# Probabilities and queries of the DRAM exchange read together, and a rearranged start of the attention loop

## The chip, the core and the metric

The kernel runs on one core of a Trainium2 chip. A core has five engines with instruction streams of their own: TensorE (PE in the profile; its weight loads are a row of their own, PEld), VectorE (DVE), ScalarE (ACT), GpSimd (POOL) and SyncE (SP), which only issues transfers. A transfer (DMA) is issued by SP, ScalarE or GpSimd and is carried out by 16 DMA engines that all queues share. On each engine the instructions run in the order in which they were written; between engines they wait on semaphores. The metric is the device time of one execution in microseconds (us).

## The reference

```python
x = x + L0_ffn(L0_cond(x, ...))     # an adapter product, then a layer with two of eight experts
x = x + L1_ffn(L1_cond(x, ...))     # attention, then a layer with sixteen of 64 experts

# L1_cond for 8 sequences of 128 tokens, 32 query heads, 8 key heads, head size 128
q = rope(rmsnorm(x @ Wq.T)); k = rope(rmsnorm(x @ Wk.T)); v = x @ Wv.T
kc, vc = k_cache[block_table], v_cache[block_table]   # 16 pages of 32 tokens: 512 cached keys
scores = q @ concat(kc, k).T / sqrt(128)              # 640 keys; four query heads share a key head
scores[cached keys past the sequence's length] = -1e30
o = softmax(scores) @ concat(vc, v)
return o @ Wo.T
```

All is in 32-bit floats. Time goes to the attention: the projections, 256 score products of 128 x 640, their softmax, the products with the values, and the output projection.

## The kernel before

**Units.** One sequence with one key head and its four query heads is a *unit*; there are 64. Two units of one sequence are a *step* (the code's `st`, 32 of them). The loop at the end runs one `iteration(u)` for each unit and three more; iteration u does the scores of unit u, and beside it the values of unit u-2, the output product of unit u-3, the projection of a later pair of units, and the norms and rotation of unit u+3. "Turn u" in this text is iteration u.

**A unit's way.** `project` (L261) makes queries, keys and values on TensorE, and VectorE adds the parts up (L264). ScalarE squares and sums each head (`norms`, L310), GpSimd makes 1/rms of it (`ss` L314, `rs` L316). VectorE rotates (`rotate_q`, `rotate_k`, L342 and after) with a table that GpSimd makes for each step (`make_tables`, L235; two buffers). The rotated queries and key must then be transposed: head size on the partitions. For the scores `heads_qk` (ScalarE, L906) puts them into `qkT`. For each of four heads, TensorE makes a 128 x 640 score in a PSUM bank (L837, L840; two such banks), VectorE masks it, takes the minimum and so frees the bank (L850, the row name is a custom operation), ScalarE makes the exponential and its sum (L861), VectorE the reciprocal, GpSimd the normalized probability (L867), and VectorE transposes it in blocks of 32 x 32 into the buffer `pb` (`blocks`, L872).

**The exchange through DRAM.** VectorE's transpose turns only within blocks of 32 x 32. The blocks themselves change places by a round through DRAM. The buffer `pb` of iteration u holds, for each of four quarters, 640 numbers of the four heads' probabilities of unit u (`PW`) and 160 of the rotated queries and key of unit u+2 (`XW = PW + 160`), which `blocks_qk` (L823) puts there. `exchange_out` writes it to DRAM in four transfers (L886): quarters 0 and 1 by SP, 2 and 3 by ScalarE. At the head of the next iteration, `exchange_in` on SP reads it back in two transfers: first the queries into `qkb` (L896), then the probabilities into `pT` (L899):

```python
if u + 2 in range(3, NU):
    qkb = wk1.tile([P, QD, NH * 32], F32, tag="qkb", name=f"qkb_{u + 2}")
    nc.sync.dma_start(out=qkb, in_=m[:, :, PW:])
    qkb_t[u + 2] = qkb
pT = wk1.tile([P, QD, PW], F32, tag=f"pT{u % 2}", name=f"pT_{u}")
nc.sync.dma_start(out=pT, in_=m[:, :, :PW])
```

`qkb` is used at the end of the same iteration by `heads_qk` for the next unit's scores, and `pT` by `values` (L919) at the end of the iteration after. There is one `pb` buffer: `blocks_qk` of the next iteration, which comes at its third head, waits until the write from it has landed. Units 0 to 2 take another way in part: the queries of units 0 to 2 are transposed on TensorE ahead of the loop, and iterations 0 and 1 use the memory of `pT0` and `pT1` as `pb`; the queries of unit 3, which go with iteration 1, lie in a gap of the buffer `xo` and have four transfers of their own.

**Other transfers.** SP also loads the key pages of the next step (`gather`, L196; 16 pages of 32 KB each): pages 0 to 9 in the step's first iteration and 10 to 15 in its second, three of them ahead of the exchange's read and the others behind it. GpSimd gathers the value rows by an indirect transfer (`gather_v`, L206, two an iteration) and issues the weight loads.

**Order.** The order on every engine is the order of the code (`manual_schedule`): no planner moves anything. Semaphores are set by the framework. Transfers issued by SP and ScalarE signal one of eight semaphores, in turn by the order of the code, and a transfer also waits for the one before it on the same semaphore.

**Sums.** TensorE's work is cut by forming sums of weights and inputs (fewer products of larger sums, after Strassen and Winograd). GpSimd makes most of them: of `xo` in `sums_x` (L172 to L176), of the projection's weights in `sums_q` (L166), of the output's weights in `sums_o` (L994), each in a slot "(iteration, head)" given by tables.

Of the kernel before, what the change touches and what calls it, by code (L numbers as in the profile page):

```python
# [9 lines left out]
F32 = mybir.dt.float32  # L10
I32 = mybir.dt.int32
AF = mybir.ActivationFunctionType
# [4 lines left out]
P = 128  # L17
B = 8
S = 128
# [4 lines left out]
D = 128  # L24
HKV, REP = 8, 4
NH = REP + 1
PAGES, PSIZE, NPP = 64, 32, 16
# [3 lines left out]
GH = 2  # L31
NQ = HKV // GH
HW = NH // 2 * D + D
QD = P // 32
HN = DM // 2
PW = REP * (LC + 1) * 32
XW = PW + NH * 32
# [21 lines left out]
def adaln_ffn_kernel(  # L59
# [169 lines left out]
    def make_tables(st):  # L229

        b = st % B
        t = pj.tile([P, 2, 4, D // 2], F32, tag="tab", name=f"tab_{st}", bufs=2)
        nwv = nw.rearrange("p i (t d) -> p (i t) d", t=2)
        for i, f in enumerate((cos, sin)):
            nc.gpsimd.tensor_tensor(  # L235
                t[:, i], nwv, f[:, b, :].unsqueeze(1).to_broadcast([P, 4, D // 2]), ALU.mult
            )
        tab_t[st] = t
# [64 lines left out]
    def norms(u):  # L303

        cs, b = c_t[u], units[u][0] % B
        ss = pj.tile([P, NH], F32, tag="ss", name=f"ss_{u}", bufs=5)
        sq = pj.tile([P, D], F32, tag="sq", name=f"sq_{u}")
        for h in range(NH):
            at = h // 2 * HW + h % 2 * D if h < REP else 2 * D
            nc.scalar.activation(sq, cs[:, at : at + D], AF.Square, accum_out=ss[:, h : h + 1])  # L310
        vn = pj.tile([P, D], F32, tag="vn", name=f"vn_{u}", bufs=6)
        nc.scalar.activation(vn, cs[:, 2 * HW - D :], AF.Copy, scale=down[:, b : b + 1])
        vn_t[u] = vn
        nc.gpsimd.tensor_scalar(ss, ss, 1.0 / D, eps[:, b : b + 1], ALU.mult, ALU.add)  # L314
        rs = pj.tile([P, NH], F32, tag="rs", name=f"rs_{u}", bufs=5)
        nc.gpsimd.tensor_tensor(rs, ss, mhalf, ALU.pow)  # L316
        rs_t[u] = rs
# [31 lines left out]
    def rotate(u):  # L349
        rotate_q(u)  # L350
        rotate_k(u)
# [46 lines left out]
    with ExitStack() as l0:  # L398
# [217 lines left out]
        for t in range(B):  # L616
            l0_adapter(t, True)
            if t >= 1:
                l0_turn_low(t - 1)
            l0_adapter(t, False)  # L620
            if t + 3 < B:
                l0_load(t + 3)
            if t + 2 < B:
                l0_load_x(t + 2)
            if t in (3, 4):
                load_q(t - 3)
            if 2 <= t <= 5:
                gather(0, (t - 2) * 4, (t - 1) * 4)
            elif t > 5:
                gather(1, (t - 6) * 4, (t - 5) * 4)  # L630
            if t >= 2:
                l0_turn(t - 2)

            if t == 5:
                project_whole(0, 0, 0, 1)
                norms(0)
            if t == 6:
                project_whole(0, 0, 1, 0)
            if t == 7:
                project_whole(0, 1, 1, 1)  # L640
                transpose_qk(0)
            if t >= 1:
                l0_experts(t - 1)
            l0_base(t)
            if t == 0:
                l0_rows()
            if 1 <= t <= 4:
                l0_angles(t - 1)
            if t in (3, 6):
                gather_v(t // 3 - 1, 0, LC)  # L650
            if t in (5, 6):
                make_tables(t - 5)
            if t == 4:
                project_whole(0, 0, 0, 0)
            if t == 5:
                project_whole(0, 0, 1, 1)
                sums_q(nc.vector, 0, 3, 2)
            if t == 6:
                project_whole(0, 1, 0, 1)
                rotate(0)  # L660
                norms(2)
                sums_q(nc.vector, 0, 4)
            if t == 7:
                project_whole(0, 1, 0, 0)
                norms(1)
# [2 lines left out]
        project_whole(0, 1, 1, 0)  # L668
        l0_turn(B - 2)
        rotate(1)  # L670
        l0_experts(B - 1)
        project_whole(1, 0, 0, 0)
        transpose_qk(1)
# [117 lines left out]
    with ExitStack() as l1:  # L791
# [6 lines left out]
        )  # L798

        p_t, pb_t, pT_t, den_t, o_t, oT_t, y_t = {}, {}, {}, {}, {}, {}, {}  # L800
        mask_t, px_t, qkb_t, qk_out = {}, {}, {}, {}

        def make_mask(st):
            b = st % B
# [4 lines left out]
        def new_pb(u):  # L809

            if u < 2:
                pb_t[u] = wk1.tile([P, QD, PW], F32, tag=f"pT{u}", name=f"pb_{u}")
                return
            pb_t[u] = wk1.tile([P, QD, XW], F32, tag="pb", name=f"pb_{u}")

        def blocks_qk(u, w):

            if w == 1:
                gap = xo[:, 0, 4:].rearrange("p x c s -> p (x c s)")[:, : NH * S]
                qk_out[w] = gap.rearrange("p (i f) -> p i f", i=QD)  # L820
            else:
                qk_out[w] = pb_t[w][:, :, PW:]
            nc.vector.transpose(  # L823
                qk_out[w].rearrange("p i (h a) -> p h i a", a=32),
                qk_t.pop(u).rearrange("p h t d -> p h (t d)").rearrange(
                    "p h (i a) -> p h i a", a=32
                ),
            )
# [40 lines left out]
        def blocks(u, h):  # L869

            w = (LC + 1) * 32
            nc.vector.transpose(  # L872
                pb_t[u][:, :, h * w : (h + 1) * w].rearrange("p i (j a) -> p j i a", a=32),
                p_t.pop((u, h)).rearrange("p (j i a) -> p j i a", i=QD, a=32),
            )

        def exchange_out(u):

            pb = pb_t.pop(u)
            m = dram_x.tile([QD, 32, QD, XW], F32, tag="px", name=f"px_{u}")  # L880
            w = XW if u + 2 in range(3, NU) else PW
            for i in range(QD):
                eng = nc.sync if i < QD // 2 else nc.scalar
                for n, end in ((PW, w), (0, PW)) if u == 1 else ((0, w),):
                    src = qk_out[u] if n else pb[:, :, :end]
                    (nc.sync if n else eng).dma_start(  # L886
                        out=m[:, :, i, n:end].rearrange("k b f -> b k f"),
                        in_=src[i * 32 : (i + 1) * 32],
                    )
            px_t[u] = m  # L890

        def exchange_in(u):
            m = px_t.pop(u).rearrange("k b i f -> (k b) i f")
            if u + 2 in range(3, NU):
                qkb = wk1.tile([P, QD, NH * 32], F32, tag="qkb", name=f"qkb_{u + 2}")
                nc.sync.dma_start(out=qkb, in_=m[:, :, PW:])  # L896
                qkb_t[u + 2] = qkb
            pT = wk1.tile([P, QD, PW], F32, tag=f"pT{u % 2}", name=f"pT_{u}")
            nc.sync.dma_start(out=pT, in_=m[:, :, :PW])  # L899
            pT_t[u] = pT  # L900

        def heads_qk(u):

# [48 lines left out]
        def slot(which, n):  # L952
# [21 lines left out]
            (1, 1): (T3, 0),  # L974
            (1, 2): (T3, 1),
            (2, 2): (T2, 0),
            (3, 0): (T2, 1),
            (3, 2): (T4, 0),
            (4, 0): (T4, 1),
            (7, 0): (T1, 0),  # L980
            (7, 1): (T1, 1),
        }
# [1 line left out]
        def sums_o(u, h):  # L984
# [11 lines left out]
        SUMS_X = {  # L996
            (0, 1): ((2, 0),),
            (0, 2): ((2, 1),),
            (6, 0): ((3, 0),),
            (7, 0): ((3, 1),),  # L1000
            (8, 0): ((0, 0),),
            (8, 1): ((0, 1),),
            (8, 2): ((1, 0),),
# [12 lines left out]
        def sums_w(u, h):  # L1016

            if u < 16:
                for i in SUMS_X.get((u, h), ()):
                    sums_x(*i)  # L1020
                do = {(3, 1): (0, 1), (4, 1): (1, 3), (4, 2): (1, 2), (5, 1): (1, 4), (5, 2): (1, 1)}
                if (u, h) in do:
                    sums_q(nc.gpsimd, *do[u, h])
            if u >= NU - 16:
                return
            r, g = u % 16, (u // 16 + 1) * GH
            do = {
                (11, 0): (0, 3),
                (11, 1): (0, 2),
                (11, 2): (0, 4),  # L1030
                (12, 0): (0, 1),
                (12, 2): (1, 3),
                (13, 1): (1, 2),
            }.get((r, h))
            if do is not None:
                sums_q(nc.gpsimd, g + do[0], do[1])
            if (r, h) in ((13, 1), (13, 3)):
                sums_q(nc.vector, g + 1, {1: 1, 3: 4}[h])
# [186 lines left out]
        def iteration(u):  # L1225
# [16 lines left out]
                slots = (1, 2, 6) if four else (4, 5, 3)  # L1242
            st = u // GH
            pages = on(u) and 1 < st + 1 < NQ * B
            first, end = ((0, 10), (10, NPP))[u % GH]
            if pages:
                gather(st + 1, first, first + 3)
            if on(u - 1):
                exchange_in(u - 1)
            if pages:  # L1250
                gather(st + 1, first + 3, end)
# [18 lines left out]
            for h in range(REP):  # L1270
                if on(u):
                    scores(u, h)
                    mask_exp(u, h)
                    if h > 0:
                        normalize(u, h - 1)

# [44 lines left out]
                norms(4 + u)  # L1321
            elif 5 < u + 3 < NU:
                norms(u + 3)
            if on(u):
                blocks(u, REP - 2)
                blocks(u, REP - 1)
                exchange_out(u)
# [187 lines left out]
```

## Time and profile before

| | |
|---|---|
| three runs, us | 1232.58, 1235.32, 1240.6; median 1235.32 |
| the profiled execution, us | 1228.33, of which the profile's span is 1226.5 |
| busy: TensorE, VectorE, GpSimd, ScalarE | 98%, 74%, 59%, 41% of the span |
| TensorE's granted clock | 1.0 of full speed over the whole |
| DMA | 302.71 MB, 247 GB/s on average; the 16 engines busy 73% from 120 to 200 us, 86% from 200 to 1150 us |
| the loop over units | first score at 115.4 us of the span, last at 1150.8 us |
| TensorE busy by stretch | 73.13 of the 80 us from 120 to 200; 942.28 of the 950 us from 200 to 1150 |

The busy times are the profile's first part. A row of a timeline gives the start in us from the span's start, the duration in us of the group from its first to its last instruction, the engine (SPq and ACTq are the instructions with which SP and ScalarE issue transfers), line, operation, output and input by their names in the program, and, in brackets, the idle time before it with what ended that. A row of the waits gives who waited (engine, output, line) for whom, then the total in us, how many times, and the longest.

### The profile page before, as it was taken

To read this page: it belongs to the slowest core of one execution; us is meant where nothing else is said; L and a number is where in the kernel's file an instruction comes from. 1 tells how busy PE (TensorE), PEld (TensorE's weight loads), DVE (VectorE), ACT (ScalarE), POOL (GpSimd) and SP (SyncE) were. 2 spreads that over 40 slices of the span, in tenths; PEclk is the share of its full clock that TensorE was granted. 3 is DMA by queue.
4 is the path that set the end of the run, shared out by engine and by line. 5 is a ranking of instruction groups with operands and counts; after the bars stand their busy time and mean duration, and the time that the engine had idled before them with its cause. 6 is when DMAs were issued, how large, how long until landed. Compare 5 with 4: busy or idle time off the path is not lost.

```text
span 1226.5 us, 16786 instructions
## 1 busy us (share of the span) xinstructions
PE 1202.6 (98%) x4159; PEld 709.2 (58%) x4159; DVE 909.9 (74%) x2098; ACT 503.7 (41%) x1457; POOL 721.2 (59%) x801
## 2 busy tenths in 40 slices
PE   8999989999999999999999999999999999999998
PEld 7765445565555556555556565655555555655444
DVE  2545877887988787878888787888787878876522
ACT  1344544444444444444344444444443444443211
POOL 2433868778755576677656675687556775732100
PEclk9999999999999999999999999999999999999999
DMA  8832688888888988898789888998889888888742
GB/s 306 286 101 96 205 253 251 247 272 275 261 245 251 280 259 237 294 288 287 236 263 294 281 231 270 297 289 248 246 257 287 262 255 262 263 260 235 219 126 97
DMA packets 206836, 302.71 MB, mean 247 GB/s; under 512 B 84819, under 2 KB 120404, under 8 KB 205844
## 3 DMA queue, kind: packets, MB, share of 16 engines
q1 hardware_dynamic: 174964, 208.72, 53.9%
q10 hardware_dynamic: 18720, 52.32, 15.9%
q0 software_dynamic: 13056, 40.60, 9.8%
q8 instruction: 33, 0.54, 0.2%
q14 instruction: 63, 0.52, 0.1%
HBM read 185.64 MB, written 115.93 MB: 246 GB/s over the span
## 4 chain that ended last, share of the span: by engine, by line
PE 68%; DMA 12%; DVE 6%; POOL 5%; issue 3%; SPq 3%; ACT 2%; ACTq 0%; DVEq 0%; POOLq 0%
PE o L919 15%; PE p L261 14%; PE s L837 12%; PE y L1044 10%; DMA px<-pb 9%; PE s L840 3%; PE bp L548 2%; PE op L1402 2%; DVE pb L872 2%; PE cp L526 2%; PE y L1057 2%; POOL p L867 2%; PE fz L733 2%; PE p L294 2%; POOL wqkv L166 1%
## 5 line engine op out<-in xcount | busy, mean ns | idle before, releaser
L861 ACT ACTIVATE p<-p,low 128x640 f32<-128x640 f32 x256 | 211.6, 827 | 463.1 <-DVE den L866 300.9
L867 POOL TENSOR_SCALAR p<-p,den 128x640 f32<-128x640 f32 x256 | 208.6, 815 | 270.2 <-DVE den L866 268.8
L261 PE MATMUL p<-wqkv,xo 128*128 128x384 f32 x784 | 282.3, 487 | 5.1 <-DVE c L264 4.9
L850 DVE CUSTOM_DVE_ANT_0 p<-s,mask,rs 128x640 f32<-128x640 f32 x256 | 222.0, 878 | 78.8 <-PE s L840 77.9
L837 PE MATMUL s<-kt,qkT 128*128 128x512 f32 x504 | 259.2, 596 | 8.5 <-DVE low L850 3.3
L919 PE MATMUL o<-pT,vt 128*128 128x512 f32 x512 | 230.2, 592 | 0.0
L872 DVE STREAM_TRANSPOSE pb<-p 128x640 f32<-128x640 f32 x256 | 211.0, 825 | 18.7 <-POOL p L867 18.7
L1044 PE MATMUL y<-wo,oT 128*128 128x256 f32 x784 | 206.6, 380 | 0.1
L261 PEld LDWEIGHTS p<-wqkv,xo 128*128 128x128 f32 x784 | 147.8, 190 | 75.9 <-DVE c L264 10.1
L840 PEld LDWEIGHTS s<-qkT 128*128 128x128 f32 x504 | 95.8, 190 | 120.5 <-issue 120.5
L206 POOL DMA_INDIRECT vt<-in_vc,vrow x128 | 143.3, 1120 | 33.8 <-issue 31.8
L919 PEld LDWEIGHTS o<-pT,vt 128*128 128x128 f32 x512 | 97.3, 190 | 110.3 <-issue 95.2
L837 PEld LDWEIGHTS s<-kt,qkT 128*128 128x128 f32 x504 | 93.4, 190 | 82.3 <-issue 34.3
L1044 PEld LDWEIGHTS y<-wo,oT 128*128 128x128 f32 x784 | 131.8, 191 | 8.9 <-PE s L840 0.2
L310 ACT ACTIVATE sq<-c 128x128 f32<-128x128 f32 x320 | 98.8, 309 | 8.1
L840 PE MATMUL s<-qkT 128*128 128x128 f32 x504 | 96.8, 274 | 0.0
L823 DVE STREAM_TRANSPOSE pb<-ca 128x640 f32<-128x640 f32 x60 | 50.3, 839 | 52.5 <-DMA px<-pb 51.5
L316 POOL TENSOR_TENSOR rs<-ss,mhalf 128x5 f32<-128x5 f32 x64 | 83.1, 1298 | 5.3
L942 ACT COPY oT<-o 128x512 f32<-128x512 f32 x64 | 37.5, 585 | 90.7 <-PE o L919 67.4
L919 PE MATMUL o<-pT,vn 128*128 128x512 f32 x128 | 65.4, 592 | 0.0
L314 POOL TENSOR_SCALAR ss<-ss,eps 128x5 f32<-128x5 f32 x64 | 21.6, 338 | 74.2 <-ACT sq L310 74.2
L264 DVE TENSOR_TENSOR c<-c,p 128x384 f32<-128x384 f32 x84 | 44.8, 534 | 22.5 <-PE p L261 22.4
(193 smaller groups left out, 1415.0 us busy)
## 6 DMA issues: line engine op xcount, KB each, us to landing
pT<-px SPq DMA_DIRECT2D x64, 1280.0 KB
px<-pb ACTq DMA_DIRECT2D x120, 400.0 KB
px<-pb SPq DMA_DIRECT2D x120, 400.0 KB
qkb<-px SPq DMA_DIRECT2D x61, 320.0 KB
kt<-in_kc SPq DMA_DIRECT2D x512, 32.0 KB
wqkv<-in_wqkv POOLq DMA_DIRECT2D x32, 384.0 KB, 5.3
wo<-in_wo POOLq DMA_DIRECT2D x17, 512.0 KB, 6.2
yd<-yp SPq DMA_DIRECT2D x12, 512.0 KB
```

The costliest lines, as they stand in the source:

```text
L206: nc.gpsimd.indirect_dma_start(out=kv_t[step][1][:, c, :], out_offset=None, in_=vc, in_offset=bass.IndirectOffsetOnAxis(ap=vrow[:, hf, at ...
L261: nc.tensor.matmul(out=ps, lhsT=xo[:, pr, x, c, :], rhs=w[:, c, :], start=(c == 0), stop=(c == 1))
L310: nc.scalar.activation(sq, cs[:, at : at + D], AF.Square, accum_out=ss[:, h : h + 1])
L316: nc.gpsimd.tensor_tensor(rs, ss, mhalf, ALU.pow)
L837: nc.tensor.matmul(out=s[:, :L], lhsT=qkT[:, h, :], rhs=kt[:, :, g % GH, :], start=True, stop=True)
L840: nc.tensor.matmul(out=s[:, L:NK], lhsT=qkT[:, h, :], rhs=qkT[:, REP, :], start=True, stop=True)
L850: nc.vector.tensor_tensor_reduce(out=p, in0=s_t.pop((u, h))[:, :NK], in1=mask_t[st], scale=rs_t[u][:, h : h + 1], scalar=BIG, op0=ALU.add, ...
L861: nc.scalar.activation(p, p, AF.Exp, bias=low, scale=-1.0, accum_out=den)
L867: nc.gpsimd.tensor_scalar(p_t[u, h], p_t[u, h], den, 1.0, ALU.mult, ALU.mult)
L872: nc.vector.transpose(pb_t[u][:, :, h * w : (h + 1) * w].rearrange("p i (j a) -> p j i a", a=32), p_t.pop((u, h)).rearrange("p (j i a) -> ...
L919: nc.tensor.matmul(out=o, lhsT=vt[:, c, j * D : (j + 1) * D] if c < LC else vn_t.pop(u), rhs=pT[:, c], start=(c == 0), stop=(c == LC),)
L1044: nc.tensor.matmul(out=y_t["y"][:, half * HN : (half + 1) * HN], lhsT=part(key)[:, i * S : (i + 1) * S], rhs=wo_t[:, slot(w, key[0] // (B ...
```

## The change

It has five parts.

1. *One read.* The tiles `pT0` and `pT1` become 800 numbers wide per quarter instead of 640. From unit 4 on `exchange_in` reads a unit's probabilities and the queries beside them by one transfer; `qkb` is now a view of `pT`. For units 1 to 3 there are still two transfers, queries first, into the two parts of the tile. The buffer `qkb` is gone.
2. *Unit 1's queries.* Since the early `pb` tiles are wide too, the queries that go with iteration 1 lie beside its probabilities. The gap in `xo` and its four own transfers are gone.
3. *Memory.* To make room, the tables have one buffer instead of two, so the second table is made behind `rotate(1)`; and the squares, whose sums alone are wanted, are written into the tile `vn` and overwritten there, so that `sq` is gone.
4. *The start of the loop.* Unit 0's last two block transposes, its write and its read move from the ends of iteration 0 and the head of iteration 1 to behind the first score, mask and exponential of iteration 1. In iterations 2 and 3 the pages are split 6 and 10 instead of 10 and 6.
5. *GpSimd's sums.* Most of the first 16 iterations' sums go a slot or two later; the four of the output's weights, the five of the projection's, and one half of a sum of `xo`.

```diff
@@ make_tables
-        t = pj.tile([P, 2, 4, D // 2], F32, tag="tab", name=f"tab_{st}", bufs=2)
+        t = pj.tile([P, 2, 4, D // 2], F32, tag="tab", name=f"tab_{st}")
@@ norms
-        sq = pj.tile([P, D], F32, tag="sq", name=f"sq_{u}")
+        vn = pj.tile([P, D], F32, tag="vn", name=f"vn_{u}", bufs=6)
         for h in range(NH):
             at = h // 2 * HW + h % 2 * D if h < REP else 2 * D
-            nc.scalar.activation(sq, cs[:, at : at + D], AF.Square, accum_out=ss[:, h : h + 1])
-        vn = pj.tile([P, D], F32, tag="vn", name=f"vn_{u}", bufs=6)
+            nc.scalar.activation(vn, cs[:, at : at + D], AF.Square, accum_out=ss[:, h : h + 1])
         nc.scalar.activation(vn, cs[:, 2 * HW - D :], AF.Copy, scale=down[:, b : b + 1])
@@ ahead of the loop
-            if t in (5, 6):
-                make_tables(t - 5)
+            if t == 5:
+                make_tables(0)
...
         rotate(1)
+        make_tables(1)
@@ new_pb
-                pb_t[u] = wk1.tile([P, QD, PW], F32, tag=f"pT{u}", name=f"pb_{u}")
+                pb_t[u] = wk1.tile([P, QD, XW], F32, tag=f"pT{u}", name=f"pb_{u}")
@@ blocks_qk
-            if w == 1:
-                gap = xo[:, 0, 4:].rearrange("p x c s -> p (x c s)")[:, : NH * S]
-                qk_out[w] = gap.rearrange("p (i f) -> p i f", i=QD)
-            else:
-                qk_out[w] = pb_t[w][:, :, PW:]
             nc.vector.transpose(
-                qk_out[w].rearrange("p i (h a) -> p h i a", a=32),
+                pb_t[w][:, :, PW:].rearrange("p i (h a) -> p h i a", a=32),
@@ exchange_out, exchange_in
+        def width(u):
+            return XW if u + 2 in range(3, NU) else PW
+
         def exchange_out(u):
-            pb = pb_t.pop(u)
+            pb, w = pb_t.pop(u), width(u)
             m = dram_x.tile([QD, 32, QD, XW], F32, tag="px", name=f"px_{u}")
-            w = XW if u + 2 in range(3, NU) else PW
             for i in range(QD):
                 eng = nc.sync if i < QD // 2 else nc.scalar
-                for n, end in ((PW, w), (0, PW)) if u == 1 else ((0, w),):
-                    src = qk_out[u] if n else pb[:, :, :end]
-                    (nc.sync if n else eng).dma_start(
-                        out=m[:, :, i, n:end].rearrange("k b f -> b k f"),
-                        in_=src[i * 32 : (i + 1) * 32],
-                    )
+                eng.dma_start(
+                    out=m[:, :, i, :w].rearrange("k b f -> b k f"),
+                    in_=pb[i * 32 : (i + 1) * 32, :, :w],
+                )
             px_t[u] = m
         def exchange_in(u):
-            m = px_t.pop(u).rearrange("k b i f -> (k b) i f")
-            if u + 2 in range(3, NU):
-                qkb = wk1.tile([P, QD, NH * 32], F32, tag="qkb", name=f"qkb_{u + 2}")
-                nc.sync.dma_start(out=qkb, in_=m[:, :, PW:])
-                qkb_t[u + 2] = qkb
-            pT = wk1.tile([P, QD, PW], F32, tag=f"pT{u % 2}", name=f"pT_{u}")
-            nc.sync.dma_start(out=pT, in_=m[:, :, :PW])
-            pT_t[u] = pT
+            m, w = px_t.pop(u).rearrange("k b i f -> (k b) i f"), width(u)
+            pT = wk1.tile([P, QD, XW], F32, tag=f"pT{u % 2}", name=f"pT_{u}")
+            for n, end in ((0, w),) if u > 3 or w == PW else ((PW, w), (0, PW)):
+                nc.sync.dma_start(out=pT[:, :, n:end], in_=m[:, :, n:end])
+            if w == XW:
+                qkb_t[u + 2] = pT[:, :, PW:]
+            pT_t[u] = pT[:, :, :PW]
@@ SUMS_O_FIRST
-            (3, 0): (T2, 1),
-            (3, 2): (T4, 0),
-            (4, 0): (T4, 1),
+            (3, 1): (T2, 1),
+            (4, 0): (T4, 0),
+            (4, 1): (T4, 1),
@@ SUMS_X
-            (6, 0): ((3, 0),),
-            (7, 0): ((3, 1),),
+            (7, 0): ((3, 0), (3, 1)),
@@ sums_w
-                do = {(3, 1): (0, 1), (4, 1): (1, 3), (4, 2): (1, 2), (5, 1): (1, 4), (5, 2): (1, 1)}
+                do = {(3, 2): (0, 1), (4, 2): (1, 3), (5, 1): (1, 2), (5, 2): (1, 4), (6, 0): (1, 1)}
@@ iteration
-            first, end = ((0, 10), (10, NPP))[u % GH]
+            some = 6 if u < 4 else 10
+            first, end = ((0, some), (some, NPP))[u % GH]
             if pages:
                 gather(st + 1, first, first + 3)
-            if on(u - 1):
+            if on(u - 1) and u > 1:
                 exchange_in(u - 1)
...
                     mask_exp(u, h)
+                    if u == 1 and h == 0:
+                        blocks(0, REP - 2)
+                        blocks(0, REP - 1)
+                        exchange_out(0)
+                        exchange_in(0)
...
-            if on(u):
+            if on(u) and u > 0:
                 blocks(u, REP - 2)
                 blocks(u, REP - 1)
                 exchange_out(u)
```

More of the change, by code (lines that the diff above doesn't have):

```diff
@@ L800, in adaln_ffn_kernel @@
         p_t, pb_t, pT_t, den_t, o_t, oT_t, y_t = {}, {}, {}, {}, {}, {}, {}
-        mask_t, px_t, qkb_t, qk_out = {}, {}, {}, {}
+        mask_t, px_t, qkb_t = {}, {}, {}
         def make_mask(st):
```

## The prediction

> **What bounds the kernel now.** First the page's busy table, then TensorE's timeline for its gaps, then the waits of all engines and of SP's queue, then the timelines of one iteration.
>
> ```profile
> PE 1202.6 (98%) x4159; PEld 709.2 (58%) x4159; DVE 909.9 (74%) x2098; ACT 503.7 (41%) x1457; POOL 721.2 (59%) x801
> ```
>
> TensorE has 1226.5 - 1202.6 = 24 us of gaps, so little can be won. In its timeline 8.2 us of them lie between 103 and 189 us, where the attention loop starts (the largest two are below), and 7.3 us after 200 us, in pieces under 1 us.
>
> ```profile
> 128.90 1.13 PE L837 MATMUL s<-kt,qkT 128*128 128x512 f32 x2 [1.55 <-DVE low L850]
> ...
> 164.46 1.56 PE L261 MATMUL p<-wqkv,xo 128*128 128x384 f32 x4 [2.97 <-DVE c L264]
> ```
>
> Behind it runs a second circle that is nearly as tight: the exchange through DRAM. The waits of all engines, then those of SP's queue:
>
> ```profile
> DVE pb L823 <- DMA px<-pb: 51.5, 33, 3.6
> ...
> ACT qkT L906 <- DMA qkb<-px: 4.4, 5, 1.9
> ```
>
> ```profile
> SPq L886 <- DVE pb L872: 91.2, 33, 10.3
> SPq L886 <- DMA px<-pb: 81.9, 29, 5.0
> ```
>
> The last line is odd: SP's half of a write waits for a write. The built program says why. All transfers of SP and ScalarE signal eight semaphores in turn, and each waits for its predecessor on the same one. In most even iterations from the fourth on, SP's first half stands eight behind ScalarE's first half of the same write. Iteration 20 on SP and on ScalarE:
>
> ```profile
> 437.81 0.54 SPq L896 DMA_DIRECT2D qkb<-px  x1
> 438.78 0.52 SPq L899 DMA_DIRECT2D pT<-px  x1
> 439.83 7.76 SPq L196 DMA_DIRECT2D kt<-in_kc  x7
> 448.70 0.82 SPq L886 DMA_DIRECT2D px<-pb  x2
> ```
>
> ```profile
> 442.17 0.71 ACT L906 COPY qkT<-qkb 128x640 f32<-128x640 f32 x1
> ...
> 444.58 0.31 ACTq L886 DMA_DIRECT2D px<-pb  x1
> ...
> 447.09 0.31 ACTq L886 DMA_DIRECT2D px<-pb  x1
> ```
>
> VectorE had the data ready at 444.34; SP wrote at 448.70, and the next read left at 454.80. I call the time from one query read's issue to the next a round: 17.1 us (median) in even iterations, 15.6 in odd, 32.8 a pair, just TensorE's own 65.6 us per four (scores of unit 8 to unit 60).
>
> **The merged read.** Removed: 58 of 61 query reads as transfers of their own. The built program has one transfer of 128 rows of 12,800 B for 512 of 640 B and 512 of 2,560 B. In the packets of the trace 640 B take 32 ns, 2,560 B 102, 8,192 B 311; at that slope 12,800 B take about 485 (an estimate). Per engine 32 x (32 + 102) = 4.3 us become 8 x 485 = 3.9. The Trainium skill (DMA: Bandwidth & Descriptors, section Anatomy of one DMA) charges each transfer about 2 us fixed plus bytes over 436 GB/s, a fit for GpSimd's path: 2.7 + 5.0 us for the two, 5.8 for one, so nearly 2 us would be saved. The trace disagrees: the second is issued 0.6 us behind the first and its packets follow without a gap; both together take 6.7 us from issue to last packet. So I take 6.4, and keep 5.8 and 7.0 as ends (the 1 MB loads of 8,192 B rows at the start needed 4.1 us or more from first to last packet, a slower rate).
>
> The price: queries now arrive with the whole. Before, they landed 3.1 us after issue; the copy to qkT (L906) follows a landing by 0.4. It is then ready at 6.8 after issue. ScalarE runs in order, and behind L906 stand the norms (2.4 us), its half of the write (L886), an eviction and the next exponential; GpSimd's rs waits for the norms, VectorE's key rotation for rs, the next unit's first mask for that, and TensorE's third score of the unit for the score bank.
>
> ```profile
> 447.15 0.35 DVE L342 SCALAR_TENSOR_TENSOR ca<-c,rs,tab 128x128 f32<-128x128 f32 x1 [0.50 <-POOL rs L316]
> ...
> 448.61 0.88 DVE L850 CUSTOM_DVE_ANT_0 p<-s,mask,rs 128x640 f32<-128x640 f32 x1
> ```
>
> L342 already waits for rs, so a late L906 moves the mask one for one. The mask ends at 449.5 and the third score starts at 450.90: 1.4 us of cover. If nothing else moved, L906 would be 2.3 to 3 us late everywhere, and most units would stall by about 1 us, some 60 us in all.
>
> **What moves with it.** One transfer fewer shifts the eight semaphores. In the built program of the change, from unit 5 on, no write waits for the other half of itself: in even iterations SP's half waits for page loads just behind the read, so it can leave about 7.1 us after the read's issue instead of 10.9. ScalarE's half leaves at 6.8 + 2.4 = 9.2. The odd iterations' write took 7.4 to 9.2 us with both halves together (the latter where yd is stored); half the bytes starting later costs perhaps 0.3 us per us. Even rounds: 7.1 + 7.4 + 0.6 = 15.1; odd: 7 + 7.7 to 9.2 + 0.6 = 15.3 to 16.8. A pair is 30.4 to 31.9, below TensorE's 32.8, so the circle keeps up and delays do not accumulate. Relative to TensorE's unit start, writes land sooner by about 2 us in even iterations and 0.5 in odd ones.
>
> L906 is then late by (u mod 4 in order 0, 1, 2, 3) 1.6, 0.8, 2.4, 1.2 us: the odd rounds' small gain feeds the even iterations. Covers, by the same reading as above: about 1.5, 2.8, 2.9 or (one in three) 1.5, and 2.2. So class 0 is on the edge; with the read's scatter (6.4 to 7.9 us between the tenth and ninetieth percentile) I take 0.4 us for each of 15 units, and 0.15 for each of class 2: +8 us. Removed: the small gaps that follow a late write (397, 426, 588, 595, 884 us) 2.8 us.
>
> **Turns 0 to 2.** Unit 1's mask moves ahead of unit 0's last two transposes (1.6 us, L872 x2): the 1.55 us gap goes. What it passes: SP's and ScalarE's writes of unit 0 and its read, later by about 0.5 us; that P is used only at 146 us. Unit 1's first normalization stays put, since GpSimd is busy until 130.7, so 0.6 us remains by unit 2. There the query part drops its four own transfers and ten pages become six: the read should leave some 1.5 to 2 us before 146.89. SP's half of unit 2's write leaves near 150, not 156.82, and the 3.56 us wait of L823, with the 2.97 us gap behind it, goes. By unit 4 this is up to 5 us. But four pages move to turn 3, and the new semaphore order gives units 3 and 4, of all, the wait for ScalarE's half; unit 4's read is merged. Round by round (157, 174.7, 191 against 162.5, 176.95, 193.0) the lead shrinks; query 6 is ready at 197.8 against 196.76. I keep 2 us of the gain (0 to 5).
>
> **The rest costs nothing here.** One table buffer: the table (L235) now waits for the last rotation's L342, but two gathers (2.4 us, L206) stand between rs and table on GpSimd, and L342 ends 0.7 us after rs; without that cover, 1.4 us and the normalizations behind. Table 1 now runs at about 109.6 behind the wo loads, done near 111.0 when rotation 2 starts at 110.92: 0.1 us. Squares into vn: same engine, reader six units old. Later sums on GpSimd: each still a head ahead of its product; both (3, ·) sums at (7, 0) take 2.9 us with 3 heads to go.
>
> **Sum.** 1228.3 us (span 1226.5 and 1.8 around it) + 8 - 2.8 - 2 = 1231.5. The three runs' median is 7.0 above this profiled run, so **1238**. No change is the forecast: about 1% (12 us) is what a measurement of this kernel tells apart.
>
> **Rivals.** *The circle becomes the bound* (0.28, about 1262). In units 8, 24 and 40 SP's half did not wait for ScalarE's, and their rounds were still 17.6, 17.0, 16.4. If even rounds stay at 17 and each is lengthened 0.8 us by ScalarE's later half, odd ones at 15.6 too, a pair needs up to 34.2. It decides from 32.8: each 0.1 us above costs 29 pairs x 0.1 = 2.9 us; at 33.7 it is +26. Against it: those three units also carry weight loads. *The read is quick enough* (0.22, about 1226). At 5.8 us all covers hold: nothing added, 2.8 to 5 removed, 4 kept at the start: -7 to -9 on the median. For it: fewer packets when the queues are busiest. Against: the bytes remain. That the read is not one transfer is excluded by the build.
>
> **Numbers.** Forecast 0.50 at 1238 (1231 to 1247), the circle 0.28 (1247 to 1275), the quick read 0.22 (1219 to 1231, about half below 1223). So faster by over 1%: 0.11; within: 0.61; slower: 0.28. Range 1222 to 1262.
>
> **What would show it.** Right: SP's waits for px writes at the write line falling from 82 us to under 20; L823's 51.5 falling; ScalarE's L906 waiting for the read in most units, 1 to 2.5 us each; gaps under 1 us before third scores of every fourth unit; the gaps at 128.9 and 164.5 gone. Wrong: even rounds at 17 us or more (circle), L906 waiting under 0.5 us (quick read), or a large new wait for the tables or for GpSimd's sums.

## The result, and the profile after

The changed kernel takes 1301.94 us (median of five, 1297.56 to 1303.99) beside 1233.54 us of the kernel before: a ratio of 1.0528, 95% interval 1.0498 to 1.0559. It is slower by 5%; the forecast was no change, at 1238, and the slow rival was put at 1262. In its profiled execution the span is 1299.8 us, 73.3 more than before.

The busy row and the chain that ended last, from the page of the changed kernel:

```profile
PE 1225.6 (94%) x4159; PEld 710.5 (55%) x4159; DVE 911.6 (70%) x2098; ACT 513.5 (40%) x1457; POOL 713.3 (55%) x801
...
DMA 48%; PE 23%; ACT 12%; POOL 8%; DVE 4%; issue 3%; ACTq 1%; SPq 1%; DVEq 0%; POOLq 0%
DMA pT<-px 24%; DMA px<-pb 23%; ACT vn L310 7%; PE s L832 3%; ACT qkT L902 3%; PE o L915 3%; PE bp L547 2%; PE op L1403 2%; PE p L261 2%; PE cp L525 2%; PE y L1052 2%; PE y L1039 2%; POOL rs L315 2%; PE fz L733 2%; PE p L294 2%
```

The same part of the page before:

```profile
PE 68%; DMA 12%; DVE 6%; POOL 5%; issue 3%; SPq 3%; ACT 2%; ACTq 0%; DVEq 0%; POOLq 0%
```

The chain ran through TensorE for 68% of the span; now it runs for 48% through transfers, half of that the read (pT<-px) and half the write (px<-pb), and for 10% through ScalarE's copy and squares. The waits of all engines and of SP's queue, after:

```profile
POOL ss L313 <- ACT vn L310: 200.1, 61, 12.5
ACT qkT L902 <- DMA pT<-px: 132.6, 54, 4.2
...
DVE ca L341 <- POOL rs L315: 121.1, 52, 3.9
...
PEld s L832 <- DVE low L845: 53.5, 47, 2.9
...
PEld s L832 <- ACT qkT L902: 37.3, 28, 3.8
...
DVE pb L818 <- DMA px<-pb: 34.4, 23, 3.7
```

```profile
SPq L882 <- DVE pb L867: 157.6, 36, 11.2
SPq L893 <- DMA px<-pb: 128.6, 71, 5.6
...
SPq L882 <- DMA px<-pb: 2.3, 1, 2.3
```

SP's wait for the other half of its own write is gone as predicted (81.9 to 2.3 us), and the copy to qkT (L902, L906 before) waits 132.6 us for the read instead of 4.4. But now the read itself (L893) waits 128.6 us for a write; before, the query read waited 42.2 us and the other read (L899) 12.6:

```profile
SPq L896 <- DMA px<-pb: 42.2, 44, 4.6
```

TensorE stands still in two places: over units 6 to 61 it is idle 17 us in all before first scores, where it mostly waits for qkT, and 25 us before third scores, where it waits for a score bank (L845); before, it was 4.5 and 0.1 us. The chain in iteration 21 shows the loop; columns are start, duration, what:

```profile
479.58 6.53 DMA pT<-px
...
486.13 0.73 ACT qkT L902
486.86 0.31 ACT vn L310 x2
...
488.94 0.02 ACT vn L311
...
489.00 0.31 ACTq L882
...
489.35 10.25 DMA px<-pb
...
499.68 7.03 DMA pT<-px
```

Read, copy, squares, ScalarE's half of the write, next read: from 479.58 to 499.68 it is 20.1 us, with no TensorE in it. In this iteration yd is stored beside; here is the whole loop as means over iterations 6 to 59, in us from the read's issue:

| kernel | copy starts | SP's half leaves | ScalarE's half leaves | its last packet | next read (round) |
|---|---|---|---|---|---|
| before | 4.1 | 8.8 | 7.1 | 13.7 (SP's 14.9) | 16.4 |
| changed | 6.9 | 7.7 | 9.8 | 17.0 (SP's 13.4) | 17.5 |

A round of 17.5 beside TensorE's 16.4 is 1.1 us lost per unit, some 64 us in 58 units. It is lost in the odd iterations alone: their rounds rose from 15.3 to 17.9 us, while the even ones stayed near 17 (17.5 before, 17.1 now). Before, a half of the write left late in even iterations only (SP's, at 10 to 11 us); now ScalarE's half is late, at 9.6 to 10.1, in every iteration. The trace agrees with the sum: the changed kernel is 6 us behind when unit 6 begins, 31 at unit 24, 50 at unit 40, 68 at unit 56.

### The profile page after: what moved, and what is told of

Same layout as the page of the kernel before. It is cut to its first block, busy times and chain, and to the rows that moved or that the text cites. A ratio compares the mean times of both kernels' runs of the same rounds, so it can differ in the third digit from the quotient of the medians.

```text
span 1299.8 us, 16765 instructions
## 1 busy us (share of the span) xinstructions
PE 1225.6 (94%) x4159; PEld 710.5 (55%) x4159; DVE 911.6 (70%) x2098; ACT 513.5 (40%) x1457; POOL 713.3 (55%) x801
## 4 chain that ended last, share of the span: by engine, by line
DMA 48%; PE 23%; ACT 12%; POOL 8%; DVE 4%; issue 3%; ACTq 1%; SPq 1%; DVEq 0%; POOLq 0%
DMA pT<-px 24%; DMA px<-pb 23%; ACT vn L310 7%; PE s L832 3%; ACT qkT L902 3%; PE o L915 3%; PE bp L547 2%; PE op L1403 2%; PE p L261 2%; PE cp L525 2%; PE y L1052 2%; PE y L1039 2%; POOL rs L315 2%; PE fz L733 2%; PE p L294 2%
## 5 line engine op out<-in xcount | busy, mean ns | idle before, releaser
L832 PE MATMUL s<-kt,qkT 128*128 128x512 f32 x504 | 266.4, 610 | 47.7 <-DVE low L845 25.3
L845 DVE CUSTOM_DVE_ANT_0 p<-s,mask,rs 128x640 f32<-128x640 f32 x256 | 220.5, 878 | 37.4 <-PE s L835 36.5
L832 PEld LDWEIGHTS s<-kt,qkT 128*128 128x128 f32 x504 | 90.0, 190 | 137.8 <-DVE low L845 51.7
L206 POOL DMA_INDIRECT vt<-in_vc,vrow x128 | 138.0, 1078 | 35.7 <-issue 31.8
L1039 PEld LDWEIGHTS y<-wo,oT 128*128 128x128 f32 x784 | 132.9, 192 | 17.8 <-POOL wo L990 8.8
L341 DVE SCALAR_TENSOR_TENSOR ca<-c,rs,tab 128x128 f32<-128x128 f32 x64 | 23.5, 368 | 121.1 <-POOL rs L315 121.1
L310 ACT ACTIVATE vn<-c 128x128 f32<-128x128 f32 x320 | 99.4, 311 | 8.1
L902 ACT COPY qkT<-pT 128x640 f32<-128x640 f32 x61 | 44.2, 725 | 132.6 <-DMA pT<-px 132.6
L315 POOL TENSOR_TENSOR rs<-ss,mhalf 128x5 f32<-128x5 f32 x64 | 77.2, 1207 | 5.3
```

Source lines behind the costliest of these rows:

```text
L206: nc.gpsimd.indirect_dma_start(out=kv_t[step][1][:, c, :], out_offset=None, in_=vc, in_offset=bass.IndirectOffsetOnAxis(ap=vrow[:, hf, at ...
L310: nc.scalar.activation(vn, cs[:, at : at + D], AF.Square, accum_out=ss[:, h : h + 1])
L832: nc.tensor.matmul(out=s[:, :L], lhsT=qkT[:, h, :], rhs=kt[:, :, g % GH, :], start=True, stop=True)
L845: nc.vector.tensor_tensor_reduce(out=p, in0=s_t.pop((u, h))[:, :NK], in1=mask_t[st], scale=rs_t[u][:, h : h + 1], scalar=BIG, op0=ALU.add, ...
L1039: nc.tensor.matmul(out=y_t["y"][:, half * HN : (half + 1) * HN], lhsT=part(key)[:, i * S : (i + 1) * S], rhs=wo_t[:, slot(w, key[0] // (B ...
```

## The experiments

Ratios are to the kernel before on the same chip. "Rounds" are means as in the table.

**Which part: the split read restored, and the reads of before swapped.**

```diff
 a_split (on the changed kernel)
-            for n, end in ((0, w),) if u > 3 or w == PW else ((PW, w), (0, PW)):
+            for n, end in ((0, w),) if w == PW else ((PW, w), (0, PW)):
 b_swap (on the kernel before)
                 qkb = wk1.tile([P, QD, NH * 32], F32, tag="qkb", name=f"qkb_{u + 2}")
-                nc.sync.dma_start(out=qkb, in_=m[:, :, PW:])
                 qkb_t[u + 2] = qkb
             pT = wk1.tile([P, QD, PW], F32, tag=f"pT{u % 2}", name=f"pT_{u}")
             nc.sync.dma_start(out=pT, in_=m[:, :, :PW])
+            if u + 2 in range(3, NU):
+                nc.sync.dma_start(out=qkb, in_=m[:, :, PW:])
```

> The changed kernel with the read split again for all units, queries first; all else of the change stays. Circle theory (the read's end, the copy L902, the norms, ScalarE's half of the write and its landing, the next read: 17.5 us a round in the changed kernel where TensorE needs 16.4): the copy runs 2.7 us earlier, ScalarE's half leaves at about 7.1 us after the read instead of 9.6, rounds fall to 16.4, and the time to that of before or 2 to 5 us below it: 1225 to 1234. Rival, that the start, the sums or the single buffers cost the time: it stays at 1290 or above.

> The kernel before with its two reads in the other order, the probabilities first and the queries second: the same packets and bytes, the queries land with the end of the exchange as in the change. Circle theory: ScalarE's half leaves 2.7 us later, and the time rises like that of the change: 1290 to 1310. Rival, that the packets of 12,800 B slow the shared DMA engines: no rise, 1232 to 1242.

The split read gave 1250.29 us, 1.0131 (1.0102 to 1.016): most of the loss is the merging, but 1.3% is not, and the expected 1225 to 1234 was missed. The swapped reads gave 1312.7 us, 1.0637 (1.0603 to 1.067): with packets as small as ever, and with no other part of the change, late queries alone make the whole loss, a little more than the 1290 to 1310 expected. Large packets are not needed for it. The copy to qkT waits there as in the changed kernel:

```profile
ACT qkT L907 <- DMA qkb<-px: 182.4, 58, 5.5
```

It starts at 7.7 us, ScalarE's half leaves at 10.1, and the round is 17.8.

**Taking ScalarE's half out from behind the squares, two failed ways.**

```diff
 a_ahead (the write ahead of the norms)
-            if u < 2: norms(4 + u)
-            elif 5 < u + 3 < NU: norms(u + 3)
             if on(u) and u > 0:
                 blocks(u, REP - 2); blocks(u, REP - 1); exchange_out(u)
+            if u < 2: norms(4 + u)
+            elif 5 < u + 3 < NU: norms(u + 3)
 a_sp (all four transfers on SP)
-                eng = nc.sync if i < QD // 2 else nc.scalar
-                eng.dma_start(
+                nc.sync.dma_start(
```

> The changed kernel, read still merged, but the last blocks and the write ahead of the norms in the code, so that ScalarE issues its half before the squares. Circle theory: ScalarE's half leaves at about 7.8 us after the read instead of 9.6, rounds near 16, and most of the loss is gone though the queries land as late as before: 1232 to 1255. Rival, that late queries stall TensorE on the direct way (copy, norms, rs, key rotation, mask), about 1 us in every unit, without the circle: no gain, since rs comes another 0.5 us later: 1300 to 1320.

> The changed kernel with all four write transfers issued by SP, none by ScalarE. Circle theory: nothing of the write stands behind the norms any more; all four leave at about 7.5 us, land about 7.5 us later, rounds near 15.7: 1228 to 1250. Rival, the direct way: 1295 to 1305, since the queries and the norms come when they came. Rival, that the exchange is short of DMA throughput: no gain either, 1295 or above.

Both missed: 1310.04 us, 1.0635 (1.0601 to 1.0668), and 1306.34 us, 1.0599 (1.0553 to 1.0645). By themselves they would have spoken for the direct way, and the second also for a shortage of DMA throughput. The traces say why neither relieved anything. With the write ahead, the squares stand behind VectorE's last block, which ScalarE's write waits for:

```profile
471.28 0.84 ACTq L882 DMA_DIRECT2D px<-pb  x2
472.17 0.31 ACT L310 ACTIVATE vn<-c 128x128 f32<-128x128 f32 x1 [1.46 <-DVE pb L867]
```

1/rms then ends 3.3 us after the unit's first score (0.3 in the kernel before, 2.6 in the changed kernel), the third score comes 6.0 us after the first (5.0 and 5.6), and that delays the last block again: another loop, through VectorE and GpSimd (20% of the chain each, transfers 11%), of 17.7 us. TensorE's idle time is now all before third scores: 49 us in units 6 to 61, none before first scores. With all four on SP the write left at 7.7 us but its last packet came at 17.0, as late as in the changed kernel: the fourth of the transfers was issued only at 10.1 us, and all four took 9.3. Each edit relieved one loop and left or closed another of the same length.

**The pair that decides.** The norms are cut in two, so that 1/rms is early in both kernels: squares, copy to qkT, [pad], value copy, ScalarE's half. The two kernels differ by eight squares whose result is dropped.

```diff
 a_nf1: PAD = 0; a_pad: PAD = 8 (both on the changed kernel)
-            if u + 1 in range(3, NU):          # ahead of the norms
-                heads_qk(u + 1)
...
-                norms(u + 3)
+                late = norms(u + 3, True)      # squares and 1/rms; the value copy comes later
+            if u + 1 in range(3, NU):
+                heads_qk(u + 1)
+            if late is not None:
+                for _ in range(PAD):
+                    late[0]()                  # a square of 128 x 128 into vn
+                late[1]()                      # the value copy into vn
```

> The changed kernel, read merged, ScalarE in the order squares, copy to qkT, eight more squares of 128 x 128 whose result is dropped (about 2 us, added work), then its half of the write: 1/rms is early again and only the write's half is late, leaving 9.6 us or more after the read as in the change. Circle theory (the half of the write is what binds): 1285 to 1310. Rival, the direct way (norms, rs, mask) binds and the write's lateness is harmless: 1240 to 1260.

> The changed kernel, read merged, ScalarE in the order squares, copy to qkT, value copy, its half of the write; it is the kernel with eight more squares without these squares. Circle theory: the half leaves at about 7.8 us after the read instead of 10.2, the copy ends at 7.4 instead of waiting behind the write, so the time is that of the copy at the end or a little less: 1236 to 1246. Rival, that the place of the copy and not the half's lateness made the loss: near 1309.

With eight squares 1309.2 us, 1.0602 (1.0552 to 1.0652), as expected; without them 1230.03 us, 0.9979 (0.9955 to 1.0003), better than the 1236 to 1246 expected. The squares took 2.4 us a unit (ScalarE is busy 647.6 us with them and 510.7 without), and cost 79 us. At most 22 us of that are 13 stretches of 3.4 us at half of TensorE's clock, of which the kernel without them has two. The waits and the chain of the kernel with eight squares:

```profile
DVE pb L823 <- DMA px<-pb: 102.2, 46, 4.4
PEld s L837 <- ACT qkT L907: 80.9, 38, 4.5
...
DVE ca L346 <- POOL rs L319: 3.0, 2, 2.5
...
DMA 45%; PE 25%; ACT 10%; DVE 10%; issue 4%; POOL 4%; ACTq 1%; SPq 0%; DVEq 0%; POOLq 0%
```

and of the one without:

```profile
DVE pb L823 <- DMA px<-pb: 20.2, 16, 3.0
PEld s L837 <- ACT qkT L907: 16.1, 19, 2.8
...
DVE ca L346 <- POOL rs L319: 3.5, 3, 2.5
...
PE 71%; DMA 16%; DVE 5%; POOL 2%; issue 2%; ACT 2%; SPq 1%; ACTq 0%; DVEq 0%; POOLq 0%
```

The direct way (rs) is free in both, so it isn't what costs here. ScalarE's half leaves at 10.2 and 7.8 us, the round is 17.9 and 16.3. With eight squares the loop through ScalarE's half of the write binds, and its round sets TensorE's first scores (L837 waits for qkT): 51 us of idle time in units 6 to 61 stand before first scores, 0.5 before third. The squares also hold up the exponential behind them, but the chain runs through the transfers. Neither large packets nor a shortage of throughput is the cause: without the squares the same merged reads and the same writes keep up.

So each of the two ways from the late copy can make a loss of this size: the write's half behind the squares here, the late norms in a_ahead. In the changed kernel both are late at once, and TensorE's stops lie on both; its chain runs through the write's loop. How the loss divides between the two there is not shown.

A third order, with the copy behind the write, agrees:

```diff
 a_last (on the changed kernel)
-            if u + 1 in range(3, NU):
-                heads_qk(u + 1)
...
                 exchange_out(u)
+            if u + 1 in range(3, NU):
+                heads_qk(u + 1)
```

> The changed kernel, read merged, with the copy to qkT moved to the end of ScalarE's iteration: norms, ScalarE's half of the write, then the copy that waits for the read. Order theory (nothing of the merged read hurts but what stands behind the copy on ScalarE): ScalarE's half leaves at about 7 us after the read, rs is as early as before, so the time falls to that of the split read, 1240 to 1258. Rival, that the queries themselves come too late for the next unit's first score: the first scores wait for qkT and it stays above 1275.

1243.95 us, 1.0065 (1.0037 to 1.0093); the copy starts at 9.0 us and TensorE's weight loads wait 60.1 us in all for it, the rival's mechanism at a small price.

**The start, the sums, the table.** Parts of the change alone on the kernel before (b_start: only the move of unit 0's end; b_sums: only the slots; b_tab: only the table buffer), and parts undone beside the split read (a_split_pages: ten and six pages again; a_split_old: also the old start and sums).

```diff
 a_split_pages
-            some = 6 if u < 4 else 10
-            first, end = ((0, some), (some, NPP))[u % GH]
+            first, end = ((0, 10), (10, NPP))[u % GH]
```

> The changed kernel with the split read and with ten and six pages again in iterations 2 and 3. In the split read's trace the first score of unit 4 stood still for 3.5 us with a half-speed clock behind it, and pages for it stood behind the read of iteration 3 on SP. If these pages are the cause, that gap goes, and 4 to 8 us of the 16 that the split read is above before: 1242 to 1247. If not: 1248 to 1252.

> The kernel before with unit 0's last blocks, write and read moved behind the first score, mask and exponential of iteration 1, nothing else. By the prediction's working it gives 1.5 us (the gap at 128.9 us): 1231 to 1234. Rival, that the later first write holds up the rounds after it: 1237 or above.

> The kernel before with only GpSimd's sums of the first 16 iterations in the changed slots. Prediction: no cost: 1231 to 1237. Rival, that they are the rest of the split read's loss: 1240 to 1246.

> The kernel before with only what the wide tiles need: one table buffer, squares into vn, unit 1's queries beside its probabilities; split read, old start, old page split, old sums. Prediction: these cost nothing: 1230 to 1237. Rival, that the table buffer or the four transfers fewer cost the rest of the split read's loss: 1243 to 1250.

> The kernel before with only the single table buffer and table 1 behind rotate(1). Prediction: no cost: 1231 to 1237. Rival, that it is what the split read with wide tiles lost against before (about 12 to 14 us): 1243 to 1249.

| run | us | ratio (interval) |
|---|---|---|
| b_start | 1236.42 | 1.0028 (1.0 to 1.0056) |
| b_sums | 1237.07 | 1.0023 (1.0002 to 1.0044) |
| b_tab | 1236.13 | 1.0009 (0.9987 to 1.0031) |
| a_split_pages | 1247.23 | 1.0116 (1.0066 to 1.0167) |
| a_split_old | 1248.48 | 1.0101 (1.0065 to 1.0137) |

Start and sums cost 0 to 0.6% each, the table nothing that shows; the 1.5 us that b_start should have gained did not come. The pages do what was suspected, but small. TensorE's timeline at unit 4's first score with the split read, six and ten pages:

```profile
174.53 2.05 PE L832 MATMUL s<-kt,qkT 128*128 128x512 f32 x2 [3.49 <-DMA px<-pb]
```

and with ten and six:

```profile
171.15 1.02 PE L915 MATMUL o<-pT,vn 128*128 128x512 f32 x2
172.01 1.02 PE L832 MATMUL s<-kt,qkT 128*128 128x512 f32 x2
```

The gap is gone, though the one behind L264 grew from 2.90 to 4.16 us; in the time this is 1250.3 to 1247.2, within the scatter. What is left in a_split_old is the wide tiles, the squares into vn, unit 1's queries, and the one table buffer that costs nothing alone, and it still costs 1%. The parts so far do not explain that.

**What the merged read is worth, once the order is right.** The same order on ScalarE, squares first, with old start, pages and sums: merged (a_nf1_old), split in the wide tiles (split_nf1_old), and on the kernel before (b_nf1).

> The same order on ScalarE with the merged read, and with the start, the page split and GpSimd's sums of the kernel before. If the loss of the split read lies in these three, it falls by about 10 more and may pass the kernel before: 1226 to 1238. If it lies in the single table buffer or the wide tiles: no lower than the same order without them, 1236 to 1246.

> The kernel before with ScalarE in the order squares, copy to qkT, value copy, half of the write; queries and probabilities still read apart. If the new order alone makes the gain: 1222 to 1228, as with the merged read. If it is the merged read with its other order of semaphores (no half of a write waits for the other half) that makes it: 1231 to 1237.

> The fastest kernel so far (merged read, squares first, old start, old pages, old sums) with the read split again, queries first, in the wide tiles. If the split read in the wide tiles has a cost of its own: 1235 to 1250, above the kernel before with the same order on ScalarE. If the loss of the split read only came from late squares: 1222 to 1230.

Merged 1223.63 us, 0.9905 (0.988 to 0.993), faster than the kernel before by 1%. Split 1242.51 us, 1.008 (1.0055 to 1.0104). The kernel before in this order 1248.49 us, 1.0129 (1.0096 to 1.0163): the order alone is a loss there, which neither expectation had. So with the squares first the merged read gains 19 us, though it moves the same bytes. Both split kernels still have SP's half waiting for a write (39.1 us in 15 waits, and 45.2 in 15 on the kernel before), the merged one has not (5.3 in 2). A last pair tests that wait by another means, the number of pages in each iteration, which also shifts the eight semaphores:

```diff
 b_pg8 (on the kernel before); nf1_pg8 likewise on a_nf1_old
-            first, end = ((0, 10), (10, NPP))[u % GH]
+            first, end = ((0, 8), (8, NPP))[u % GH]
```

> The kernel before with eight and eight pages in a step's two iterations instead of ten and six, nothing else. In the built program SP's half of the write then waits for ScalarE's half of the same write in 13 iterations instead of about 29. If that wait costs time in the split read (as in the kernel before with the squares first, and in the split read with squares first): a small gain, 1224 to 1232. If it costs nothing: 1232 to 1238.

> The fastest kernel so far (merged read, squares first, old start and sums) with eight and eight pages. Both iterations of a step then have equal page loads beside the exchange; no half of a write waits for the other in either. If the ten pages behind the read held rounds up: 1218 to 1224; if not: 1223 to 1230.

On the kernel before 1222.6 us, 0.9894 (0.9861 to 0.9927). On the merged read 1226.37 us, 0.9922 (0.9891 to 0.9952), not different from ten and six. SP's queue with eight and eight pages on the kernel before:

```profile
SPq L886 <- DVE pb L872: 94.0, 54, 10.5
SPq L196 <- DMA px<-pb: 78.2, 37, 3.7
SPq L886 <- DMA px<-pb: 56.2, 14, 6.2
```

The waits of SP's half for a write fall from 29 to 14, SP's half leaves at 7.5 us instead of 8.8, and VectorE's wait for pb (L823) falls from 51.5 to 9.3 us. The page count by itself gave nothing where there was no such wait. This edit of one line is as fast as the best merged read and simpler. That the wait is what it saved is likely but not shown: even page loads could help only beside the split read, and the wait at the write does not rank the split kernels. It is 56.2 us in 14 waits here, in the fastest of them, and 45.2 in 15 in b_nf1, one of the slowest. SP's half leaves at 8.8 to 9.0 us of the round in every kernel with the queries read first and ten and six pages, and at 7.5 to 7.9 here and in the merged ones with the squares first; but the kernel before is one of the former, and 1% faster than the slowest of them.

## Why the prediction was wrong

**The step that failed** is the one headed "What moves with it": "half the bytes starting later costs perhaps 0.3 us per us", and from it "Even rounds: 7.1 + 7.4 + 0.6 = 15.1". It let the write's 7.4 us count from SP's half. (Its 0.6 is either the price of ScalarE's later half, 2.1 us at 0.3, or the time from the last packet to the next read, 0.5 to 0.6 us in the trace; the sum has room for one of them only.) The next read needs both halves, and SP's head start hardly shortens ScalarE's half: from its own issue this takes 6.3 to 8.5 us (medians of the four classes of iterations), and 7.0 to 9.0 in a_nf1, where both leave together. The packets show it: SP's run from 8.6 to 13.4 us of the round, ScalarE's, issued at 9.8, only from 12.0 to 17.0. Its first packet comes 2.2 us after the issue, 1.3 in a_nf1; why, stays open. From SP's issue to the last packet of either half it is 9.3 us in the changed kernel and 7.9 in a_nf1: 1.4 us more for a half that leaves 2 us later, about 0.7 us per us and not 0.3. The round is 9.6 + 6.9 + 0.6 = 17.1 in iterations 0 of 4, and 18.5 in iterations 1 of 4, where yd is stored; predicted 15.1 and up to 16.8. The prediction had seen that ScalarE's half would leave at 9.2. The gain that it booked for even rounds, SP's half no longer waiting, did not come, because ScalarE's half was now nearly as late as SP's had been; and in odd rounds, where both halves had left at 6.7 to 6.9, it was a new delay of 3 us.

**The rival** "the circle becomes the bound" was right in mechanism and in its point of decision, 32.8 us a pair. Its size was off by the same term: it lengthened each round by 0.8 us, to 34.2 at most for a pair; 35.1 was measured, with the even rounds no longer than before and the odd ones longer by 2.6. At its own price, 29 pairs x (35.1 - 32.8) = 67 us, near the 73 of the traces; it was taken at 26.

**Right:** the merged read's time (6.4 us from issue to last packet; the copy at 6.9, predicted 6.8), and with it the choice of the trace over the price of a transfer in the Trainium skill (DMA: Bandwidth & Descriptors, section Anatomy of one DMA), which made it 5.8; the end of SP's wait for its own write; ScalarE's half at 9.2 (9.6 in iterations 0 and 1 of 4, 9.8 on average); L906 waiting for the read in most units (132.6 us, 54 times, 2.5 us on average, the upper end of what was forecast). The case "if nothing else moved", some 60 us from stalls before third scores, is near the number that came, but in part by luck: 25 us of TensorE's idle time stand before third scores, and a_pad lost 79 us with next to none there.

**The start** was put at 2 us gained. The trace shows 6 lost by unit 6: the 1.55 us gap at 128.9 is gone, but the gap behind L264 stays at 2.58, and a new one of 3.56 us opens at unit 4's first score, in TensorE's timeline of the changed kernel:

```profile
163.26 1.89 PE L261 MATMUL p<-wqkv,xo 128*128 128x384 f32 x4 [2.58 <-DVE c L264]
...
174.36 1.83 PE L832 MATMUL s<-kt,qkT 128*128 128x512 f32 x2 [3.56 <-DMA px<-pb]
```

The sentence on the four pages moved to turn 3 had no price: they stand behind the read of that iteration on SP. With ten and six pages (a_split_pages) the new gap was gone, and the one behind L264 larger.

**"The rest costs nothing"** holds for the table; the sums cost 0 to 0.4%. The 1% of a_split_old is a miss whose cause stays open. The wait of SP's half was read as odd and priced only through the rounds; b_pg8, which halves the number of these waits, gained 1%, though that the wait is the reason is not shown.

## What to carry to other kernels

When a transfer is merged with a later one, list what stands behind its reader on the reader's engine, and follow each item until it comes back to the transfer: here some 2 us of squares, with half of a write behind them, stood between the read and the next read, and moving them was worth 72 us (1302 to 1230). A transfer made in two halves is done when the later half is done, and here the head start of the first half won back only a third of the delay of the second. Before an edit is blamed, change the order on one engine: four orders of the same work on ScalarE gave 1230, 1244, 1302 and 1310 us.

## What was not expected of the hardware

TensorE's granted clock fell to half for 3.4 us at a time in the changed kernel, five times in the span, each time near the end of a gap of 1.5 to 3.6 us; the kernel before had none of these inside its span, though it had a gap of 2.97 us. The stretches behind the two first gaps, and one without (columns: stretch, its length, busy us of PE, PEld, DVE, ACT, POOL with instructions, granted clock, DMA share, GB/s):

```profile
164.00:167.00 3.00, 3.00 (x6) 1.51 (x5) 2.81 (x8) 2.80 (x10) 1.60 (x2) 0.56 1.03 383
174.50:177.20 2.70, 2.70 (x6) 1.56 (x7) 0.55 (x1) 0.00 (x0) 0.00 (x0) 0.52 0.90 246
205.00:208.00 3.00, 3.00 (x8) 1.33 (x7) 2.09 (x4) 1.94 (x8) 0.22 (x1) 1.00 0.52 115
```

Five times 3.4 us at half speed are at most 8.5 us of the 73. The length of a gap doesn't decide it: one of 2.92 us at 507 us had no such stretch, one of 1.54 at 795 us had.
